# Block 0's first ff product as 26 products, its weight sums on GpSimd, and a new order of the side work of five stages

## The chip, the cores and the metric

The kernel runs on one core of a Trainium2 chip. Its time is device microseconds of one execution. All data are fp32. TensorE multiplies; VectorE, ScalarE and GpSimd do the rest; the DMA queues named here are issued from SyncE (SP) and ScalarE.

## The reference

A conditioned transformer block without attention, on x of shape (2, 2048, 512), with D = 512 and H = 1024 (`t` is the conditioning vector of a sequence):

```python
emb = jnp.dot(jax.nn.silu(t), ada_w) + ada_b
shift_msa, scale_msa, gate_msa, shift_mlp, scale_mlp, gate_mlp = jnp.split(emb, 6, axis=-1)
norm = _ln(x) * (1.0 + scale_msa[:, None]) + shift_msa[:, None]
h = jax.nn.gelu(jnp.dot(norm, ssm_w1) + ssm_b1, approximate=False)
ssm_out = jnp.dot(h, ssm_w2) + ssm_b2
x = x + gate_msa[:, None] * ssm_out
norm2 = _ln(x) * (1.0 + scale_mlp[:, None]) + shift_mlp[:, None]
hf = jax.nn.gelu(jnp.dot(norm2, ff_w1) + ff_b1, approximate=True)
ff_out = jnp.dot(hf, ff_w2) + ff_b2
x = x + gate_mlp[:, None] * ff_out
```

`_ln` is a layer norm without weights (eps 1e-6). ssm_w1 and ssm_w2 are 512x512, ff_w1 is 512x1024, ff_w2 1024x512.

## The kernel before

The 4096 rows are eight blocks of 512 tokens. Each block goes through four stages of TensorE, called here hA (norm times ssm_w1), oA (times ssm_w2, and the first residual), hC (second norm times ff_w1) and oC (times ff_w2, and the second residual), with the block's number behind them. The order of the stages is written out by hand: hA_0, oA_0, hA_1, oA_1, hC_0, hA_2, oC_0, hC_1 and so on, so that the side work of one block lies beside the products of another.

**Products.** A matrix product is done with fewer multiplications than the plain one, from sums and differences of quarters of its operands. `group` (L550, matmuls L565) does it with seven products, P1 to P7, in the order P1 P2 P6 P5 P7 P3 P4 (`ORDER`) or P1 P2 P5 P6 P7 P3 P4 (`FIRST`). A product of 512 x 512 quarters is four matmuls of the program, eight in the trace, and writes one of the PSUM banks y, x, v. `Second.products` (L1253, matmuls L1283) does the whole first ff product of a block in 26 products of half that size. Its operands are called registers: 28 of weights (16 pieces of ff_w1 and 12 of the room `fw1_s`, each 128x256) and some 24 of tokens. Two lists of sums over registers prepare them, `HK_A` (37 sums, weights, once) and `HK_B` (20 sums, tokens, per block), made by `sums_of_registers` (L1195). `HK_P` lists the products: bank, whether the bank starts afresh, the two registers, and which of the eight pieces of the result take the bank in, with signs. ScalarE reads a bank for the first time of a piece (L1297), VectorE adds to it later (L1300), and the gelu follows when a piece is complete (L1278). A bank must have been read before a product that starts it afresh or adds to it can run. Before, block 0 used `group` twice for hC_0 (14 products), and blocks 1 to 7 used `products`; the 37 weight sums were made on VectorE in hC_0, hA_2 and oC_0, after block 0 had used the plain ff_w1, and a quarter of ff_w1 that had been overwritten was loaded again (`fw1_quarter`).

**Side work.** A stage takes a table `hooks`, from the name of a product to the operations that are issued after it. What is issued goes to the queue of its engine and is done in that order. The side work is:

- `Norm`: the statistics of a block's rows, on VectorE (`stats`, L602, L603) or on ScalarE (`sums_on_act` L619, `squares_on_act` L631), then the root on GpSimd as a power (`root`, L649 to L656) with refinement steps (`rest`, L658 and L696 to L704 on VectorE, L671 on GpSimd), the normal form (`normal`, L719, ScalarE), turning by VectorE within 32x32 blocks (`turn`, L730) and a move of 16 DMA pieces of 64 KB (`move`, L739), the scale and shift of the conditioning (`modulate`, L767 on ScalarE, L769 on VectorE), and the sums of its quarters (`summed`, L386).
- The sums of the rows of a stage's result for the next one (`First.summed`, `Second.summed`; they use `cut_sum`, L386).
- The rows of emb: TensorE makes them (L287), VectorE shapes them (L329, L333), and the gates go to DRAM and come back (`store_gates` L364, `load_gate` and `take_gate` L374). The gate is multiplied into the rows of the second weight (`weight_of_second`, folds L434) and into its bias (`gb5_0` L1501), and seeds put the bias into PSUM (L529).

What sets the order near the change is this hand-written list, for the first stages, of what hangs on which product (L1443 to L1640).

Of the kernel before, what the change touches and what calls it, by code (L numbers as in the profile page):

```python
# [45 lines left out]
    (1, '-', 1, 0),  # L46
    (3, '+', 3, 1),
    (11, 'n', 10, 11),
    (27, '+', 11, 1),
    (26, '-', 27, 8),  # L50
    (25, '+', 13, 15),
    (25, '-', 25, 12),
    (24, '-', 27, 2),
    (23, '-', 3, 24),
    (8, '+', 8, 23),
    (8, '+', 0, 8),
    (22, '-', 12, 26),
# [51 lines left out]
    (5, True, 26, 20, ((5, -1), (7, 1))),  # L109
# [3 lines left out]
    (5, False, 8, 21, ((1, 1),)),  # L113
# [22 lines left out]

HK_BANK = {5: "y", 2: "x", 4: "v", 0: "x", 1: "y", 3: "v"}
# [3 lines left out]
def kernel(  # L141
# [447 lines left out]
    class Norm:  # L589
# [17 lines left out]
        def mixed_stats(self):  # L607

            sums, var = self.sums_on_act(), self.squares_on_act(D**-0.5)
            return sums[:3] + var[:4], self.stats(self.mv)[3:]  # L610

        def sums_on_act(self):
# [3 lines left out]
            self.unread = work.tile([P, C, D], F32, tag="blocks", name=f"unread{n}")  # L616
# [109 lines left out]
        def turn(self, c):  # L726
# [6 lines left out]
            )  # L733

# [460 lines left out]
    def sums_of_registers(program, reg, engs, copied=None, beside=()):  # L1195


        def op(n, d, f, a, b):
# [4 lines left out]
            elif f == "n":  # L1203
                nc.vector.scalar_tensor_tensor(reg[d], reg[a], -1.0, reg[b], ALU.mult, ALU.subtract)
            else:
                eng.tensor_tensor(reg[d], reg[a], reg[b], ALU.add if f == "+" else ALU.subtract)  # L1206
# [36 lines left out]
    class Second:  # L1243
# [9 lines left out]
        def products(self, fa, fb, hooks, act_first=False):  # L1253


            ends = {b: n for n, (b, *_) in enumerate(HK_P)}
            starts = [(n, b) for n, (b, fresh, *_) in enumerate(HK_P) if fresh]
            stops = set(ends.values())
            for n, b in starts:
                stops |= {max([m for m in range(n) if HK_P[m][0] == b], default=ends[b])}  # L1260
# [4 lines left out]
            left = [sum(d == r for (*_, rs) in HK_P for r, _ in rs) for d in range(8)]  # L1265
# [15 lines left out]
            for n, (b, fresh, ra, rb, reads) in enumerate(HK_P):  # L1281
# [171 lines left out]
    def gb2_0():  # L1453
        nc.vector.tensor_tensor(b2_bc, gate[2, 0], b2_bc, ALU.mult)

    def fold2(lo, hi):
        return [lambda k=k: found["w2"][1][k]() for k in range(lo, hi)]

    hooks = {}
    hook(hooks, ("P1",), n1_sums[2:3])  # L1460
    on_act, on_dve = n1[1].mixed_stats()
    hook(hooks, ("P1",), on_act)
    hook(hooks, ("P6",), on_dve + [n1[1].root, lambda: gate_rows_of(2)] + n1_sums[3:])
    hook(hooks, ("P6",), [n1[1].rest] + [lambda c=c: n1[1].normal(c) for c in range(2)])
    hook(hooks, ("P7",), [ssm_gate, gb2_0, lambda: seed("oA_0", b2_bc, 0), lambda: apart_row(b2_bc, nc.gpsimd)] + fold2(0, 1))
    hook(hooks, ("P3",), fold2(1, 2) + [lambda: n1[1].turn(0)] + fold2(2, 4))
    hook(hooks, ("P3",), fold2(4, 7) + [lambda: seed("oA_0", b2_bc, 1)])

    def later_loads():
        load_ada(5)  # L1470
        load_gate_b(5)
        load_w("fw2", fw2, fw2_sb)

    hA[0] = First(0, n1[0].ops, hooks, FIRST, hA_0)
    w2_ops = found["w2"][0]

    hA_sums = hA[0].summed(nc.vector, nc.gpsimd)
    n1[1].normal(2)
    n1[1].normal(3)
    run([hA_sums[0], lambda: n1[1].turn(1), hA_sums[1]])  # L1480
    hooks = {}
    hook(hooks, ("P1",), [lambda: n1[1].turn(2), lambda: n1[1].turn(3), lambda: n1[1].move((nc.sync, nc.scalar)), later_loads])
    hook(hooks, ("P1",), fold2(7, 8) + hA_sums[2:])
    hook(hooks, ("P1",), [lambda: found.update(pada=rows_of(3))])
    hook(hooks, ("P2",), [lambda: modulation(3, 0, found["pada"])])
    hook(hooks, ("P6",), [lambda: found.update(pada=rows_of(4))])
    hook(hooks, ("P4",), [lambda: modulation(3, 1, found["pada"])])
    hook(hooks, ("P7",), n1[1].moved((None, nc.vector)))
    n2 = {0: Norm(0, 2)}
    fw1_ops, fw1_sums, fw1_s = weight_of_first("fw1", fw1_sb)  # L1490
    hook(hooks, ("P2",), fw1_sums[:1])
    def ff_gate():
        take_gate(5, 0)
        gb[5] = load_row(work.tile([P, D], F32, tag="gb5", name="gb5_0", bufs=1), fb2)
        found["fw2"] = weight_of_second(fw2_sb, fw2_s, gate[5, 0], (nc.vector,), 4)

    def fold5(lo, hi):
        return [lambda k=k: found["fw2"][1][k]() for k in range(lo, hi)]

    def gb5_0():  # L1500
        nc.vector.tensor_tensor(gb[5], gate[5, 0], gb[5], ALU.mult)  # L1501
        apart_row(gb[5], nc.gpsimd)

# [4 lines left out]
    residual("oA_0", 0, hA[0], w2_ops, KD // 2, hooks, order=FIRST)
    run(st[2:])
    hooks = {}  # L1510
    hook(hooks, ("P1",), n1_sums[2:3])
    hook(hooks, ("P2",), n1_sums[3:] + on_dve + [n2[0].root])
    hook(hooks, ("P6",), [n2[0].rest] + [lambda c=c: n2[0].normal(c) for c in range(C)])
    hook(hooks, ("P5", "P7"), [lambda p=p: seed("oA_1", gb[2], p) for p in range(2)])
    hook(hooks, ("P5", "P7"), fw1_sums[1:3])
    hook(hooks, ("P6",), [lambda: gate_rows_of(5)])
    hook(hooks, ("P6", "P7", "P7", "P7"), [lambda c=c: n2[0].turn(c) for c in range(C)])
    hook(hooks, ("P7",), [lambda: n2[0].move((nc.sync,), (0, 1)), lambda: store_gates(5), lambda: load_gate(5, 0), lambda: store_gates(2)])
    load_x(2)
    hA[1] = First(1, n1[1].ops, hooks, FIRST)  # L1520

    n2[0].move((nc.scalar,), (2, 3))
    hA_sums = hA[1].summed(nc.vector)
    run(hA_sums[:2])
    n1[2] = Norm(2, 1)
    st = n1[2].stats()
    hooks = {}
    hook(hooks, ("P1",), hA_sums[2:3])  # L1530
    hook(hooks, ("P2",), hA_sums[3:] + fw1_sums[3:])
    hook(hooks, ("P2", "P6", "P6", "P5"), st)
    hook(hooks, ("P6",), n2[0].moved() + [ff_gate])
    n2_sums = n2[0].summed(nc.gpsimd)
    hook(hooks, ("P5",), n2_sums[:1] + [n1[2].scales])
    hook(hooks, ("P7",), n2_sums[1:] + [lambda c=c: n1[2].normal(c) for c in range(C)])
    hook(hooks, ("P7", "P3"), fold5(0, 2))
    turns = [lambda c=c: n1[2].turn(c) for c in range(C)]
    residual("oA_1", 1, hA[1], w2_ops, KD // 2, hooks)


# [392 lines left out]
```

## Time and profile before

| | us |
|---|---|
| median of 3 runs | 577.80 (577.78 to 578.07) |
| profiled execution | 577.74 |
| its span | 575.9 |
| hC_0, block 0's first ff product | 24.35 (68.19 to 92.54) |
| hC_1, block 1's, by 26 products | 22.45 (128.80 to 151.25) |

The page gives the busy time of each engine as a share of the span, the chain of work that ended last, and groups of instructions by line and tile. In a row of the timeline the first number is the start, the second the busy time of the row, both in us, then engine, line, operation, output from input, shapes and count; in brackets stands the idle time before it and what ended it. A row of the chain has start and length. A program matmul has two instructions in the trace, so x8 is a product of 512-size quarters.

### The profile page before, as it was taken

Reading aid. Unit: us, or ns where it says so; the run is one execution under the profiler, and the core shown is the slowest. Engines: PE = TensorE matmul, PEld = TensorE weight load, DVE = VectorE, ACT = ScalarE, POOL = GpSimd, SP = SyncE. Lnnn points to the kernel's source line nnn. Section 1 sums busy time; section 2 is a strip of 40 time slices with the busy share of each in tenths; the row PEclk is TensorE's granted clock in tenths of the full one; section 3 lists DMA queues with packets and bytes.
Section 4 is the critical chain, followed back from the end, with each engine's and each line's share of the span. In section 5 each row is a group of like instructions: output and inputs, shape, how many; then the busy total and the mean of one; then the engine's idle time right before and its main releaser. Section 6 shows DMA issues by size and latency. Waiting matters only on the chain.

```text
span 575.9 us, 10119 instructions
## 1 busy us (share of the span) xinstructions
PE 570.8 (99%) x3443; PEld 514.1 (89%) x3443; DVE 453.6 (79%) x963; ACT 292.7 (51%) x574; POOL 436.7 (76%) x460
## 2 busy tenths in 40 slices
PE   8999999999999999999999999999999999999997
PEld 4888888888899889998899988998889999899897
DVE  4968898996878586987869877996768598897676
ACT  3727457705652875448734588326655431742430
POOL 1665449999949869889898999998994885379361
PEclk9999999999999999999999999999999999999999
DMA  8977333303205223283032930243240240031002
GB/s 329 390 232 249 100 71 92 96 38 146 58 18 162 106 100 69 97 260 126 1 93 50 330 115 21 54 109 122 101 109 2 110 126 23 1 73 74 2 1 73
DMA packets 26863, 62.30 MB, mean 108 GB/s; under 512 B 5136, under 2 KB 6204, under 8 KB 25148
## 3 DMA queue, kind: packets, MB, share of 16 engines
q1 hardware_dynamic: 22784, 55.87, 29.9%
q10 hardware_dynamic: 4028, 5.79, 3.9%
q8 instruction: 27, 0.44, 0.4%
q14 instruction: 24, 0.20, 0.1%
HBM read 35.94 MB, written 9.97 MB: 80 GB/s over the span
## 4 chain that ended last, share of the span: by engine, by line
PE 97%; DMA 2%; SPq 0%; DVE 0%; issue 0%; DVEq 0%
PE px_hC L1283 11%; PE py_hA L565 10%; PE py_hC L1283 8%; PE pv_hC L1283 8%; PE pl_oC_P_y L1038 5%; PE py_oC L990 5%; PE pv_hA L565 5%; PE py_oA L925 5%; PE pl_oC_A_y L1133 4%; PE py_oA L565 4%; PE pl_oC_P_v L1038 3%; PE pl_oC_B_y L1133 3%; PE py_hC L565 2%; PE px_hA L565 2%; PE py_oC L565 2%; PE pl_oA_y L940 2%
## 5 line engine op out<-in xcount | busy, mean ns | idle before, releaser
L656 POOL TENSOR_TENSOR r<-ve,minus_half 128x4 f32<-128x4 f32 x16 | 16.6, 1037 | 57.7 <-DVE ve L655 50.7
L767 ACT ACTIVATE nT<-nT,mod,mod 128x512 f32<-128x512 f32 x32 | 23.4, 803 | 46.2 <-DMA nT<-blocks 16.3
L1206 POOL TENSOR_TENSOR forms<-forms 128x256 f32<-128x256 f32 x56 | 42.5, 759 | 3.8 <-DVE forms L1202 0.4
L1283 PE MATMUL py_hC<-forms,fw 128*128 128x256 f32 x168 | 40.9, 379 | 0.0
L1300 DVE TENSOR_TENSOR hClo<-hClo,py_hC 128x512 f32<-128x512 f32 x42 | 28.5, 683 | 11.6 <-ACT hClo L1297 8.2
L719 ACT ACTIVATE nT<-x,nmr,rstd 128x512 f32<-128x512 f32 x36 | 26.8, 803 | 19.4 <-DVE nmr L704 16.8
L1283 PEld LDWEIGHTS py_hC<-forms,fw 128*128 128x128 f32 x168 | 31.7, 190 | 4.6 <-DVE hClo L1300 0.2
L386 POOL TENSOR_TENSOR hSC<-hClo,hChi 128x512 f32<-128x512 f32 (+1 forms) x16 | 19.2, 1205 | 18.7 <-ACT hChi L1278 17.9
L602 DVE BATCH_NORM_STATS2 st<-x 128x6 f32<-128x512 f32 x42 | 28.4, 675 | 4.9 <-DMA x<-in_x_dram 4.9
L1300 DVE TENSOR_TENSOR hChi<-hChi,pv_hC 128x512 f32<-128x512 f32 x35 | 23.2, 678 | 9.2 <-PE pv_hC L1283 5.0
L1278 ACT ACTIVATE hClo<-hClo,colsT 128x256 f32<-128x256 f32 x56 | 25.3, 498 | 5.0 <-DVE hClo L1300 4.8
L1283 PE MATMUL px_hC<-forms,fw 128*128 128x256 f32 x112 | 27.6, 379 | 0.0
L767 ACT ACTIVATE x<-x,mod 128x512 f32<-128x512 f32 x24 | 17.5, 801 | 18.8 <-DMA x<-blocks 18.8
L386 POOL TENSOR_TENSOR hClo<-hClo 128x512 f32<-128x512 f32 (+1 forms) x23 | 26.5, 1154 | 0.0
L1278 ACT ACTIVATE hChi<-hChi,colsT 128x256 f32<-128x256 f32 x56 | 25.1, 496 | 1.9 <-DVE hChi L1300 1.9
L730 DVE STREAM_TRANSPOSE blocks<-nT 128x512 f32<-128x512 f32 x36 | 24.2, 695 | 1.7 <-ACT nT L719 1.7
L1297 ACT ACTIVATE hChi<-py_hC 128x512 f32<-128x512 f32 x14 | 7.6, 594 | 34.0 <-PE py_hC L1283 14.8
L1297 ACT ACTIVATE hClo<-px_hC 128x512 f32<-128x512 f32 x21 | 12.5, 596 | 22.5 <-PE px_hC L1283 18.9
L1283 PEld LDWEIGHTS px_hC<-forms,fw 128*128 128x128 f32 x112 | 21.3, 190 | 2.9
L565 PE MATMUL py_hA<-x,w 128*128 128x256 f32 x96 | 22.7, 379 | 0.0
L1300 DVE TENSOR_TENSOR hChi<-hChi,px_hC 128x512 f32<-128x512 f32 x28 | 19.1, 682 | 4.3 <-ACT hClo L1297 2.1
L1283 PE MATMUL px_hC<-forms,fw_s 128*128 128x256 f32 x84 | 20.5, 380 | 0.0
(537 smaller groups left out, 1921.9 us busy)
## 6 DMA issues: line engine op xcount, KB each, us to landing
x<-in_x_dram SPq DMA_DIRECT2D x13, 1024.0 KB
out_dram<-x SPq DMA_DIRECT2D x14, 512.0 KB
x<-blocks SPq DMA_DIRECT2D x96, 64.0 KB
nT<-blocks SPq DMA_DIRECT2D x88, 64.0 KB
ada<-in_L_cond_ada_w_dram SPq DMA_DIRECT2D x5, 1024.0 KB
fw<-in_L_cond_ff_w_dram SPq DMA_DIRECT2D x2, 2048.0 KB
nT<-blocks ACTq DMA_DIRECT2D x56, 64.0 KB
w<-in_L_cond_ssm_w_dram SPq DMA_DIRECT2D x2, 1024.0 KB
```

Of the source, the lines that this page charges most:

```text
L386: eng.tensor_tensor(out[:, r], a[:, r], b[:, r], f)
L565: nc.tensor.matmul(ps[b][j * apart][:, j, :], lhs(p, j, k), rhs(p, j, k), start=(fresh and j * (not apart) == 0 and k == 0), stop=(p in (" ...
L602: nc.vector.bn_stats(st, xs[self.i][:, c, :])
L767: nc.scalar.activation(dst, src, AF.Identity, bias=shift, scale=scale)
L925: nc.tensor.matmul(ps[BANK[p]][:, j, :], hops(p, j, k), wops[p][:, k, :], start=False, stop=(k == KD // 2 - 1), skip_group_check=True,)
L990: yield lambda j=j, k=k: nc.tensor.matmul(ps[BANK[p]][:, j, :], hops(p, j, k), wops[p][:, k, :], start=False, stop=(k == kdim - 1), skip_g ...
L1038: nc.tensor.matmul(t[:, n, :], hops.leaves[p][f][:, k, :], leaf_wops[p][f][:, k, :], start=room not in started, stop=(f in ("P2", "P3", "P ...
L1133: nc.tensor.matmul(rooms[g, b][:, at[p], :], hops.leaves[p][f][:, k, :], leaf_wops[p][f][:, k, :], start=(g, b) not in started, stop=(f in ...
L1206: eng.tensor_tensor(reg[d], reg[a], reg[b], ALU.add if f == "+" else ALU.subtract)
L1278: nc.scalar.activation(h, h, AF.Gelu_apprx_tanh, bias=fb1T[:, m : m + 1])
L1283: nc.tensor.matmul(ps[b][:, j, :], fa[ra][:, j * P : (j + 1) * P], fb[rb].rearrange("p a (c q) -> p c a q", q=Q), start=(fresh and j == 0) ...
L1300: nc.vector.tensor_tensor(dest(d), dest(d), ps[b], op)
```

## The change

Block 0's ff product is done with `products` too. The signs in `HK_A`, `HK_B` and `HK_P` are changed so that no sum is of the form -a-b (which VectorE alone could do, L1204), so that any engine can make any sum. `HK_P0` is `HK_P` in another order, for block 0. The 37 weight sums move ahead of hC_0, to oA_0, hA_1, oA_1 and hC_0: five on VectorE (the first four and the last), 32 on GpSimd. The token sums of block 0 are made in oA_1 and hC_0, four on VectorE and 16 on GpSimd. The reload of ff_w1's quarter and the four Strassen sums of ff_w1 go.

The hooks of six stages are no longer written as calls but as a table `PLAN`, stage to product to names of operations, and a table `BY`, name to engines, a letter for each operation (V, A, G for VectorE, ScalarE, GpSimd). Moves are split at the pieces `ON_SCALAR` between SP and ScalarE's queue. The statistics of block 0's second norm are cut into parts (`split_stats`). The last steps for block 2's first norm move from GpSimd to VectorE (`root`), its sums stay on GpSimd, and one of its four statistics goes to ScalarE. Gate 5's rows are taken into use in hC_0, at product 15, and its folds are in hC_0 and hA_2; the sums of ff_w2 and of the hidden rows of block 0 are in hA_2. The second norm of block 1 is modulated, and its token sums begin, in oC_0.

```diff
 HK_A = [
-    (1, '-', 1, 0),
-    (3, '+', 3, 1),
-    (11, 'n', 10, 11),
+    (1, '-', 0, 1),
+    (3, '-', 1, 3),
+    (11, '+', 10, 11),
...
+HK_P0 = [HK_P[n] for n in (1, 0, 2, 6, 9, 4, 5, 3, 8, 11, 7, 12, 13, 14, 15, 10, 16, 19, 18, 17, 20, 22, 21, 23, 25, 24)]
+PLAN = {
+    "hA_0": {
+        "start": "n1_0.sum.0 n1_0.sum.1",
+        "P1": "n1_1.stats.0 n1_1.stats.1 n1_1.stats.2 n1_1.stats.3 n1_0.sum.2 n1_1.stats.6",
+        "P2": "n1_1.stats.4 n1_1.stats.5",
+        "P6": "n1_1.stats.7 n1_1.root.0 gate_2.0 n1_0.sum.3 n1_1.rest.0 n1_1.normal.0",
...
+        "P3": "w2.1 w2.2 n1_1.turn.0 w2.3 w2.4 w2.6 w2.5",
+        "P4": "n1_1.normal.1 n1_1.normal.3 n1_1.normal.2 seed_0.1",
+    },
+    "oA_0": {
+        "start": "hA_0.sum.0 rows.0 n1_1.turn.1 hA_0.sum.1",
...
+        "P5": "a.0",
+        "P6": (
+            "rows.1 a.1 a.2 a.3 a.4 a.5 a.6 a.7"
+            " a.8 a.9 a.11 a.12 mods.0"
+        ),
+        "P7": "n1_1.modulated.0 n1_1.modulated.1 mods.1 n1_1.modulated.3 n1_1.modulated.2",
...
+    "hA_1": {
+        "start": "a.14 n2_0.stats.4 n2_0.stats.3 n2_0.stats.6 n2_0.stats.7",
+        "P1": "a.13 a.15 seed_1.1 seed_1.0 n2_0.stats.8 n2_0.root.0",
+        "P2": "n1_1.sum.2 a.16 a.17 a.18 a.19 a.21 a.22 a.23",
+        "P6": (
+            "a.20 n2_0.rest.0 n2_0.normal.0 n2_0.normal.1 n2_0.normal.2 gates.0 rows.2 n2_0.normal.3"
+            " n1_1.sum.3"
+        ),
+        "P7": "a.24 n2_0.turn.0 n2_0.turn.1",
+        "P3": "n2_0.turn.2 n2_0.turn.3 gates.1 n2_0.move.0",
+        "P4": "a.26 n1_2.stats.0",
+    },
+    "oA_1": {
+        "start": "hA_1.sum.0 a.29 hA_1.sum.2 n1_2.stats.1 n2_0.move.1",
+        "P1": "hA_1.sum.1 n1_2.stats.2 gates.2 a.28 n1_2.stats.4 n1_2.stats.3 hA_1.sum.3",
+        "P6": "n1_2.stats.5 n1_2.root.0",
+        "P5": "a.25 n2_0.modulated.0",
+        "P7": (
+            "n2_0.modulated.1 n2_0.modulated.2 n2_0.modulated.3 copies.0 b.0 b.2 b.1 b.3"
+            " b.4 b.6 b.5 b.7"
+        ),
+        "P3": (
+            "b.8 b.9 b.10 b.11 b.13 n1_2.rest.0 b.15 b.12"
+            " a.27 a.31 b.16 b.17 a.30 a.32"
+        ),
+        "P4": "table.0",
+    },
+    "hC_0": {
+        0: "n1_2.normal.0 a.33 b.14",
+        1: "n1_2.turn.0 n1_2.normal.1",
+        2: "b.19 n1_2.normal.3",
+        3: "b.18 n1_2.normal.2 n1_2.turn.1",
+        4: "a.34",
+        5: "n1_2.turn.2",
+        6: "n1_2.turn.3",
+        7: "a.35",
+        8: "n1_2.move.1 n2_1.stats.0 n1_2.move.0",
+        9: "a.36",
...
+        15: "ff_gate.0",
...
+        19: "fw2.0 n1_2.modulated.2 n1_2.modulated.1 n1_2.sum.0 n1_2.sum.2 n1_2.sum.1",
+        20: "n1_2.sum.3 fw2.4",
+        22: "n2_1.normal.0 n2_1.normal.1",
+        23: "gb_5.0 gb_5.1 fw2.1",
+        25: "n2_1.turn.0",
+    },
+    "hA_2": {
+        "start": "n2_1.normal.3",
...
+        "P6": "fw2.2 fw2.6 hC.sum.0 hC.sum.4 n2_1.turn.1 fw2.8",
+        "P5": "hC.sum.1 hC.sum.2 seed_2.1 fw2.9 hC.sum.5",
...
+BY = {
...
+    "n1_2.sum": "GGGG",
+    "hA_0.sum": "VVGG",
+    "hA_1.sum": "VVGG",
...
+    "n1_1.modulated": "AAVV",
+    "n2_0.modulated": "VAAV",
...
+    "a": "VVVVGGGGGGGGGGGGGGGGGGGGGGGGGGGGGGGGV",
+    "b": "VVVGGGVGGGGGGGGGGGGG",
+}
+BESIDE, COPIED, ON_SCALAR, ON_ACT = (17,), (1,), (8, 7, 2), ((), ('P5',))
...
-            self.early = (self.i, self.which) in ((2, 1), (1, 2))
+            self.early = (self.i, self.which) == (1, 2)
...
+        def move_some(self, eng, pieces):
+            for a, m in pieces:
+                eng.dma_start(
+                    out=self.nT[m * Q : (m + 1) * Q, a, :],
+                    in_=self.bl[a * Q : (a + 1) * Q, m].rearrange("p k c q -> p (k c q)"),
+                )
...
+    residual("oA_0", 0, hA[0], w2_ops, KD // 2, begin("oA_0"), order=FIRST)
+    hooks = begin("hA_1")
+    hA[1] = First(1, n1[1].ops, hooks, FIRST, on_act=ON_ACT[0])
+    residual("oA_1", 1, hA[1], w2_ops, KD // 2, begin("oA_1"))
+    hooks = begin("hC_0")
+    hC.products(fa, fb[0], hooks, True, HK_P0)
```

In the table, `a` are the weight sums in the order of `HK_A`, `b` the token sums in that of `HK_B`, `n1_1` is block 1's first norm, `n2_0` block 0's second, `w2` and `fw2` the folds and sums of the second weights, `loads` and `gates` DMAs.

More of the change, by code (lines that the diff above doesn't have):

```diff
@@ L1264, in products @@
             }
-            left = [sum(d == r for (*_, rs) in HK_P for r, _ in rs) for d in range(8)]
+            left = [sum(d == r for (*_, rs) in products for r, _ in rs) for d in range(8)]
             fresh_dest, done = set(range(8)), []
@@ L1451, in ssm_gate, with rows_for @@
         found["w2"] = weight_of_second(w2_sb, w2_s, gate[2, 0], (nc.vector,))
[L1453 to L1491, printed above, removed]
+    def rows_for(g):
+        found[g] = rows_of(g)
     def ff_gate():
@@ L1508 @@
[L1508 to L1517, printed above, removed]
@@ L1533 @@
[L1533 to L1539, printed above, removed]
-    hC = Second(0)
-    n2[1] = Norm(1, 2)
-    hooks = {}
-    hook(hooks, ("P1", "P1", "P2"), turns)
@@ new lines @@
+    at("seed_0", lambda: seed("oA_0", b2_bc, 0), lambda: seed("oA_0", b2_bc, 1))
+    at("seed_1", lambda: seed("oA_1", b2_bc, 0), lambda: seed("oA_1", b2_bc, 1))
+    at("w2", *[lambda n=n: found["w2"][1][n]() for n in range(8)])
+    at("loads", lambda: load_ada(5), lambda: load_gate_b(5), lambda: load_w("fw2", fw2, fw2_sb), lambda: load_x(2))
+    later("hA_0.sum", 4, lambda: hA[0].summed(ENGS["hA_0.sum"]))
+    later("hA_1.sum", 4, lambda: hA[1].summed(ENGS["hA_1.sum"]))
+    at("rows", lambda: rows_for(3), lambda: rows_for(4), lambda: gate_rows_of(5))
@@ new lines @@
+    at("b", *[lambda n=n: form_0(n) for n in range(len(HK_B))])
+    at("table", lambda: nc.scalar.activation(unread, minus_half, AF.Gelu_apprx_tanh))
+    room = forms[:, 8:].rearrange("p (c n) a r -> p c (n a r)", c=C)
+    later("n1_2.stats", 6, lambda: sum(n1[2].mixed_stats(1, room), []))
+    at("n1_2.root", n1[2].root)
+    at("n1_2.rest", n1[2].rest)
+    turned("n1_2", n1[2], ON_SCALAR[2], ENGS["n1_2.normal"])
+    at("n1_2.modulated", *n1[2].moved(ENGS["n1_2.modulated"]))
+    later("n1_2.sum", 4, lambda: n1[2].summed(ENGS["n1_2.sum"]))
@@ new lines @@
+    later("n2_1.stats", 4, n2[1].stats)
+    at("n2_1.scales", n2[1].scales)
+    turned("n2_1", n2[1], 0, ENGS["n2_1.normal"])
+    at("ff_gate", ff_gate)
+    at(
+        "gb_5",
+        lambda: nc.vector.tensor_tensor(gb[5], gate[5, 0], gb[5], ALU.mult),
+        lambda: apart_row(gb[5], nc.gpsimd),
+    )
+    at("fw2", *[lambda n=n: found["fw2"][1][n]() for n in range(12)])
+    at("seed_2", lambda: seed("oC_0", gb[5], 0), lambda: seed("oC_0", gb[5], 1))
+    later("hC.sum", 8, lambda: hC.summed(0, nc.gpsimd) + hC.summed(1, nc.gpsimd))
@@ L1623 @@
         hooks = {}
-        if i == 1:
-            assert not fa_sums
         if i == 1:
```

276 lines of the change are left out of this document (158 added, 118 removed).

## The prediction

> **What bounds the kernel now.** I read the page first, then the idle time of TensorE, then the chain of waits in order of time, and after that the timeline of each other engine between 20 and 95 us.
>
> ```profile
> span 575.9 us, 10119 instructions
> PE 570.8 (99%) x3443; PEld 514.1 (89%) x3443; DVE 453.6 (79%) x963; ACT 292.7 (51%) x574; POOL 436.7 (76%) x460
> PE 97%; DMA 2%; SPq 0%; DVE 0%; issue 0%; DVEq 0%
> ```
>
> ```profile
> PE idle L1392 <- POOL w_t masks.py:199: 1.3, 1, 1.3
> PE pada L304 <- DMA ada<-in_L_cond_ada_w_dram: 0.3, 1, 0.3
> ```
>
> TensorE is 97% of the chain, and its two waits lie at the start. Every matmul less is a gain of its whole length, and every wait that the new order makes for TensorE is a loss of its whole length. Of the chain these rows matter (start, length, what):
>
> ```profile
> 42.76 1.73 PE py_hA L565 x8
> ...
> 50.68 1.92 PE py_hA L565 x8
> ...
> 59.51 1.73 PE py_oA L565 x8
> ...
> 62.96 1.73 PE py_oA L565 x8
> ...
> 68.19 1.73 PE py_hC L565 x8
> ...
> 75.10 1.90 PE py_hC L565 x8
> ...
> 92.54 1.73 PE py_hA L565 x8
> ...
> 125.35 3.45 PE py_oC L565 x16
> ...
> 151.25 1.73 PE py_oA L565 x8
> ```
>
> Block 0's first ff product runs from 68.19 to 92.54, 24.35 us in 14 products. Block 1's, already in 26 half-size products, runs from 125.35 + 3.45 = 128.80 to 151.25, 22.45 us. The sum is made against the profiled execution, 577.74 us (1.84 outside its span, taken as unchanged); the median of the runs is 577.80, 0.06 above.
>
> **1. The products.** 14 x 4 = 56 program matmuls become 26 x 2 = 52: 22.45 for 24.35, **-1.90**. Of this, 1.73 is four matmuls (one row of eight instructions) and 0.17 the long product at 75.10. It needs every sum and every bank in time; the rest of the sum goes through these.
>
> **2. Weight sums on GpSimd.** Four sums of 128x1024 go, and 37 sums of 128x256, which VectorE made between 84 and 128 us, come 50 us earlier: five on VectorE (four early, the last in the ff stage), 32 on GpSimd.
>
> ```profile
> 35.49 1.27 POOL L386 TENSOR_TENSOR hSA<-forms,hSA 128x512 f32<-128x512 f32 x1
> 36.72 2.35 POOL L386 TENSOR_TENSOR fw_s<-fw 128x1024 f32<-128x1024 f32 x1
> 48.72 1.02 POOL L656 TENSOR_TENSOR r<-ve,minus_half 128x4 f32<-128x4 f32 x1 [9.64 <-DVE ve L655]
> ```
>
> ```profile
> L1206 POOL TENSOR_TENSOR forms<-forms x56: 722/729/1195, 118.5 to 531.8; 128x256 f32<-128x256 f32 x56
> L1206 DVE TENSOR_TENSOR fw_s<-fw x4: 683/901/1377, 93.3 to 120.4; 128x256 f32<-128x256 f32 x4
> L1206 DVE TENSOR_TENSOR fw_s<-fw,fw_s x5: 833/843/950, 99.4 to 113.7; 128x256 f32<-128x256 f32 x5
> L1206 DVE TENSOR_TENSOR fw<-fw_s,fw x2: 407/428/448, 115.6 to 122.7; 128x256 f32<-128x256 f32 x2
> ```
>
> The columns are least, median and greatest ns. GpSimd's first 12 must wait for VectorE's fourth, which I place at 38.2. At 0.73 each, plus about 0.7 for VectorE's sums beside them, they end at 47.6. Behind them in GpSimd's queue stands the power for block 0's second norm (r of the row at 48.72), which then ends at 49.45, not 49.74: still no loss. Eleven more follow, and the two sums of block 1's hidden rows on GpSimd end at 59.5 and 61.5, needed at 62.96 and a product later. The last weight sum ends at about 84.4, its product is due at about 88. Cost **0** as long as a sum takes 0.73; rival C is what happens otherwise.
>
> That VectorE and GpSimd hold each other up is in these rows: 0.43 us on VectorE alone, 0.84 to 1.38 beside GpSimd. The Trainium skill, SBUF — State Buffer, section "SBUF: two separate sides", calls the port pair of the two an exclusive lock: a VectorE instruction with two SBUF inputs against a GpSimd instruction that reads SBUF, and the later one waits out the whole of the other. The trace agrees: 1.38 is 0.43 and a wait of 0.95, most of the 1.27 us of a GpSimd 128x512 sum. By that rule every such sum of VectorE may wait one GpSimd sum; rival D is that case, priced from the rows.
>
> **3. Block 1's first norm (hA_0).** ScalarE now loads its gelu table and does one gelu ahead of two squares of the statistics.
>
> ```profile
> 21.43 1.28 ACT L842 ACT_TABLE_LOAD   x1
> ...
> 41.00 1.52 ACT L767 ACTIVATE nT<-nT,mod 128x512 f32<-128x512 f32 x2 [10.42 <-DMA fw_t<-in_L_cond_ada_b_dram]
> ```
>
> ```profile
> 22.63 0.17 DVE L655 TENSOR_SCALAR ve<-mv 128x4 f32<-128x4 f32 x1
> ...
> 30.79 1.15 DVE L386 TENSOR_TENSOR hSA<-hSA,forms 128x512 f32<-128x512 f32 x1
> ...
> 32.46 1.29 DVE L730 STREAM_TRANSPOSE blocks<-nT 128x512 f32<-128x512 f32 x2
> ...
> 48.47 0.17 DVE L655 TENSOR_SCALAR ve<-mv 128x4 f32<-128x4 f32 x1
> ...
> 53.50 1.88 DVE L730 STREAM_TRANSPOSE blocks<-nT 128x512 f32<-128x512 f32 x3
> ...
> 57.38 0.69 DVE L386 TENSOR_TENSOR hSA<-hSA,hA 128x512 f32<-128x512 f32 x1
> ```
>
> ve moves from 22.63 to 23.4, the last turn ends at 34.45 instead of 33.75, the 16 pieces land 0.65 later than the 41.00 at which both engines begin to modulate. The second chunk is ready at 43.2; hA_1's first product (42.76) reaches it 0.43 in, at 43.19. **+0.1** (0 to 0.3).
>
> **4. hA_1.** ve of block 0's second norm still waits for ScalarE's last square (48.2 against 48.47 for ve before). What is new is behind it on VectorE's queue: two reads of finished products and a sum of 128x512 that the product at 50.68 needs. These end at about 50.8: **+0.15**. If the sum takes 1.15 as at 30.79 instead of 0.69, 0.65; if ScalarE is earlier, 0.
>
> **5. oA_1.** The four turns now end at 56.85 (55.38 before: 53.50 + 1.88), because VectorE's sums come before them. Behind them are two sums of the hidden rows. Before, GpSimd was idle there and the second took 0.69; now it is busy, so I take 1.15 for each: ready at 59.95, due at 59.51 plus the 0.25 lost so far. **+0.2** (0 if at 0.69; 0.9 if each waits a further 0.35).
>
> **6. The move of block 0's second norm.** It is split nine pieces on SP and seven on ScalarE's queue; gate 5's four stores now stand ahead of it on SP.
>
> ```profile
> 55.44 4.95 SPq L739 DMA_DIRECT2D nT<-blocks  x8
> 60.44 2.72 SPq L364 DMA_DIRECT2D gates<-w_t  x4
> ```
>
> ```profile
> 57.60 4.14 ACTq L739 DMA_DIRECT2D nT<-blocks  x6
> 63.29 2.93 ACT L767 ACTIVATE nT<-nT,mod,mod 128x512 f32<-128x512 f32 x4 [5.94 <-DMA gates<-w_t]
> ...
> 69.29 2.93 ACT L719 ACTIVATE x<-x,nmr,rstd 128x512 f32<-128x512 f32 x4 [1.38 <-POOL nmr L671]
> ...
> 129.76 1.09 ACT L1297 ACTIVATE hChi<-py_hC 128x512 f32<-128x512 f32 x2 [14.81 <-PE py_hC L1283]
> ```
>
> The stores take 2.72 but are issued from 52.3, while VectorE still turns: hidden. The pieces go out from 57.0 to 63.0 (0.62 each on SP, 0.69 on ScalarE's queue) and land 1.55 after the last issue, as before (57.60 + 4.14 to 63.29): 64.55 against 63.29. Two engines modulate until 66.35, four instead of 2.93 us of one. The 20 token sums, 16 of them on GpSimd with two weight sums between, follow from 66.35: with 0.73 a sum the ones due for products 6, 9 and 12 of the new order (counted from 0, the stage starting at 68.6) are ready 0.1, 0.5 and 0.7 early. **0** (0 to 0.5: at 0.84, the median row beside the other engine, the first is 0.5 late).
>
> **7. hC_0 itself.** In its first 6 us ScalarE makes two reads, the four normals of block 2's norm and two more reads: at 0.55 and 0.73 each they end 5.8 us in. VectorE's third turn waits for the last normal, and in its queue the read of product 6, whose bank product 8 overwrites, stands behind it.
>
> ```profile
> 72.74 1.28 DVE L730 STREAM_TRANSPOSE blocks<-x 128x512 f32<-128x512 f32 x2
> ...
> 130.63 1.29 DVE L1300 TENSOR_TENSOR hChi<-hChi,pv_hC 128x512 f32<-128x512 f32 x2 [0.97 <-PE pv_hC L1283]
> ```
>
> A turn and a read are 0.64 each: the read ends 7.2 to 7.3 us in, product 8 is due at 8 x 22.45 / 26 = 6.91. **+0.4** (0 if ScalarE's reads come earlier; 1.0 if another read gets between). Later banks come free in time by the same count. Gate 5's rows, its eight folds and the four fw2 sums with the eight hidden sums on GpSimd (4 x 2.35 + 8 x 1.27) now reach into hA_2 and oC_0; the first product that needs them is due 3 us after they are ready. The 512 KB reload of weights on ScalarE's queue goes, which nothing waited for. The move of block 2 has 14 of 16 pieces on SP and lands near 88, 0.4 ahead of the sum that needs it. **0** (0 to 0.6).
>
> **Sum:** 577.74 - 1.90 + 0.10 + 0.15 + 0.20 + 0.40 = 576.69, **576.7 us**. With all stalls at their low ends 575.84; with all at their high ends (0.3, 0.65, 0.9, 0.5, 1.0, 0.6) 579.8.
>
> **The rivals.**
> A is the sum above.
> B: all of it is hidden. The stalls that I foresee are each under half a microsecond and rest on hand-counted queues; an operation 0.2 us earlier removes two of them. 577.74 - 1.90 = 575.84. Against it: four places would all have to be kind.
> C, the slower side: the power for block 0's second norm falls behind the twelve weight sums. From 38.2 to the 48.45 at which it is to start is 10.25 us, 0.85 per sum. GpSimd's greatest row is 1195 ns; at 1.07, between that and the 0.95 that VectorE's sums reach, the power starts at 51.0, 2.6 late, and so do the turns, the sums of item 5, and with them oA_1: 576.7 + 2.6 = 579.3. It decides (579.3 is past +0.2%) from 2.2 us on, 1.04 per sum. For it: GpSimd has no gap there any more, where it waited 9.64 before. Against it: the median is 0.729, and VectorE has only two sums of two SBUF inputs in that time.
> D: the port waits of item 2 come in full. VectorE's sum in hA_1 waits one GpSimd sum (0.15 + 0.73), both of item 5 0.73 instead of 0.46 (0.2 + 0.54), items 3 and 7 stay (0.5): 2.12, 577.74 - 1.90 + 2.12 = 578.0.
>
> **How the numbers follow.** 0.2% is 1.16 us, about what a measurement of this kernel tells from no change: faster is below 576.6, slower above 578.9. A 0.42 (its own range 576.2 to 577.2, so half of it counts as faster), B 0.23, D 0.18, C 0.17. Faster 0.23 + 0.20 = 0.43, same 0.22 + 0.18 = 0.40, slower 0.17. The range leaves out C and ends between D and C: 575.8 to 578.7.
>
> **What would show it.** In the changed profile: 26 products of 0.86 in hC_0, 22.45 us and what stalls add; the power for block 0's second norm starting at 48.5 (C: 50.6 or later); VectorE's sums of item 5 at 1.15 (B: 0.69, D: 1.4); the modulation at 64.5; idle TensorE of 0.1 to 0.4 us at hA_1's start and its fifth product, oA_1's third, and product 8 of hC_0. The prediction is wrong if TensorE waits somewhere else, above all for token sums after 74 us, or in hA_2 and oC_0, where I count nothing.

## The result and the profile after

The changed kernel takes 579.44 us (median of 11 runs, 579.28 to 580.41), the kernel before 577.80 (11 runs): a ratio of 1.0028, 95% interval 1.0019 to 1.0037. It is 0.28% slower; the interval excludes no change, and its lower end lies just under the 0.2% that the prediction took as the limit of a measurement. The forecast was 576.7 with a range to 578.7.

The profiled execution after takes 579.28 us, 1.54 more than the one before; its page begins:

```profile
span 577.5 us, 10112 instructions
PE 569.3 (99%) x3435; PEld 512.0 (89%) x3435; DVE 439.6 (76%) x954; ACT 295.8 (51%) x585; POOL 451.0 (78%) x475
```

TensorE is busy for 1.5 us less, and yet the span is 1.6 us longer. TensorE's waits (line, what it waited for, us in total, times, longest) tell why:

```profile
PE idle L1512 <- POOL w_t masks.py:199: 1.3, 1, 1.3
PE py_hA L672 <- DVE hA L957: 1.3, 2, 1.0
PE pada L409 <- DMA ada<-in_L_cond_ada_w_dram: 0.9, 1, 0.9
PE py_oA L672 <- DVE hSA L491: 0.6, 1, 0.6
```

The first and third lie at the start, where hA_0 begins at the same time as before. The second and fourth are new. A table by stage (length, PE busy, PEld, DVE, ACT, POOL, granted clock, DMA share, GB/s) puts them in place. The stages are hA_1, oA_1, hC_0 and hA_2; first the kernel before:

```profile
42.60:55.89 13.29, 13.29 (x89) 11.37 (x88) 11.72 (x28) 9.42 (x21) 7.17 (x4) 1.00 0.78 277
55.89:68.03 12.14, 12.14 (x58) 10.56 (x56) 8.85 (x19) 4.88 (x8) 3.66 (x6) 1.00 0.45 109
68.03:92.38 24.35, 24.35 (x114) 21.20 (x112) 21.99 (x39) 15.81 (x25) 15.58 (x27) 1.00 0.27 69
92.38:104.47 12.09, 12.09 (x58) 10.64 (x57) 11.61 (x15) 7.19 (x14) 12.09 (x14) 1.00 0.41 100
```

and the same four of the kernel after:

```profile
42.88:56.54 13.66, 13.37 (x90) 11.37 (x88) 12.03 (x27) 10.38 (x24) 13.08 (x17) 1.00 0.76 276
56.54:69.48 12.94, 12.35 (x57) 10.56 (x56) 11.22 (x23) 5.96 (x12) 8.51 (x10) 1.00 0.41 103
69.48:92.58 23.10, 22.96 (x106) 19.51 (x104) 21.90 (x45) 13.51 (x25) 18.16 (x31) 1.00 0.25 57
92.58:105.91 13.33, 12.32 (x57) 10.56 (x56) 10.85 (x17) 10.75 (x21) 13.17 (x11) 1.00 0.01 1
```

hA_1 starts 0.28 later; then hA_1 +0.37, oA_1 +0.80, hC_0 -1.25, hA_2 +1.24: oC_0 starts 1.44 later, and everything behind it keeps that distance. hC_0 did win its 1.9 (22.45 and 0.65 of waits). The five stages around it (0.28 of it in hA_0 and oA_0) lost 2.69, and hC_0 itself 0.65.

The rows of VectorE after, at the places where TensorE waits:

```profile
23.31 0.17 DVE L773 TENSOR_SCALAR ve<-mv 128x4 f32<-128x4 f32 x1 [0.83 <-ACT unread L749]
23.52 0.29 DVE L446 TENSOR_TENSOR w_t<-pada,fw_t 128x128 f32<-128x128 f32 x1
...
48.23 0.57 DVE L773 TENSOR_SCALAR ve<-mv 128x4 f32<-128x4 f32 x1 [1.39 <-ACT unread L749]
...
58.47 0.69 DVE L1012 TENSOR_TENSOR x<-py_oA,x 128x512 f32<-128x512 f32 x1 [0.82 <-PE py_oA L672]
59.08 1.62 DVE L491 TENSOR_TENSOR hSA<-hSA,hA 128x512 f32<-128x512 f32 x1
...
75.54 0.70 DVE L848 STREAM_TRANSPOSE blocks<-x 128x512 f32<-128x512 f32 x1
76.17 0.65 DVE L1420 TENSOR_TENSOR hChi<-hChi,px_hC 128x512 f32<-128x512 f32 x1
```

The gate's rows (w_t) stand behind ve, which waits for ScalarE: 23.52 for 22.86. In hA_1 ve waits 1.39 for ScalarE with four steps behind it that the fifth product needs. In oA_1 the second hidden sum starts behind the read of P1 and takes 1.62. In hC_0 the read of product 6 ends at 76.8 and product 8 starts at 76.87. And the chain of waits through the start of hA_2, in order of time:

```profile
88.51 1.52 ACT x L893 x2
90.03 0.80 ACT hChi L1398 x2
90.83 1.41 ACT x L893 x2
92.24 0.80 ACT hClo L1398 x2
93.04 0.80 ACT hChi L1398 x2
93.84 0.71 ACT nT L837
...
94.58 0.71 DVE blocks L848
95.29 1.17 DVE nT L841
96.46 0.61 DVE hA L957
...
97.20 1.97 PE py_hA L672 x8
```

The read of P1 (L957) was free to start at about 94.4, when P1 was done. It stands behind a turn (L848), which waits for ScalarE's normal form, and behind a normal form on VectorE (L841).

### The profile page after: what moved, and what is told of

Read it like the earlier page. It is cut to its first block, busy times and chain, and to the rows that moved or that the text cites. A ratio compares the mean times of both kernels' runs of the same rounds, so it can differ in the third digit from the quotient of the medians.

```text
span 577.5 us, 10112 instructions
## 1 busy us (share of the span) xinstructions
PE 569.3 (99%) x3435; PEld 512.0 (89%) x3435; DVE 439.6 (76%) x954; ACT 295.8 (51%) x585; POOL 451.0 (78%) x475
## 4 chain that ended last, share of the span: by engine, by line
PE 90%; DMA 2%; SPq 2%; DVE 2%; ACT 2%; issue 0%; DVEq 0%; ACTq 0%
PE px_hC L1403 11%; PE py_hA L672 9%; PE py_hC L1403 9%; PE pv_hC L1403 9%; PE pl_oC_P_y L1164 5%; PE py_oC L1116 5%; PE py_oA L1051 4%; PE pv_hA L672 4%; PE pl_oC_A_y L1259 4%; PE pl_oC_P_v L1164 3%; PE pl_oC_B_y L1259 3%; PE py_oA L672 3%; PE py_oC L672 2%; PE pl_oA_y L1066 2%; SPq L856 2%; PE pl_oC_A_v L1259 2%
## 5 line engine op out<-in xcount | busy, mean ns | idle before, releaser
L1330 POOL TENSOR_TENSOR forms<-forms 128x256 f32<-128x256 f32 x64 | 47.9, 749 | 6.5 <-DVE forms L1330 2.3
L1403 PE MATMUL py_hC<-forms,fw 128*128 128x256 f32 x192 | 46.7, 379 | 0.0
L1403 PEld LDWEIGHTS py_hC<-forms,fw 128*128 128x128 f32 x192 | 36.3, 190 | 5.2 <-DVE hClo L1420 0.2
L491 POOL TENSOR_TENSOR hSC<-hClo,hChi 128x512 f32<-128x512 f32 x14 | 18.2, 1302 | 18.6 <-ACT hChi L1398 17.8
L1403 PE MATMUL px_hC<-forms,fw 128*128 128x256 f32 x128 | 31.5, 379 | 0.0
L1398 ACT ACTIVATE hClo<-hClo,colsT 128x256 f32<-128x256 f32 x64 | 28.8, 498 | 5.0 <-DVE hClo L1420 4.8
L1398 ACT ACTIVATE hChi<-hChi,colsT 128x256 f32<-128x256 f32 x64 | 28.7, 496 | 3.8 <-DVE hChi L1420 3.8
L848 DVE STREAM_TRANSPOSE blocks<-nT 128x512 f32<-128x512 f32 x36 | 24.2, 694 | 1.9 <-ACT nT L837 1.9
L1403 PE MATMUL px_hC<-forms,fw_s 128*128 128x256 f32 x96 | 23.6, 382 | 0.1
L1403 PE MATMUL pv_hC<-nT,fw 128*128 128x256 f32 x96 | 23.3, 379 | 0.0
L1420 DVE TENSOR_TENSOR hClo<-hClo,px_hC 128x512 f32<-128x512 f32 x26 | 17.6, 677 | 7.0 <-PE px_hC L1403 6.6
```

The source lines that it names most:

```text
L491: eng.tensor_tensor(out[:, r], a[:, r], b[:, r], f)
L1398: nc.scalar.activation(h, h, AF.Gelu_apprx_tanh, bias=fb1T[:, m : m + 1])
L1403: nc.tensor.matmul(ps[b][:, j, :], fa[ra][:, j * P : (j + 1) * P], fb[rb].rearrange("p a (c q) -> p c a q", q=Q), start=(fresh and j == 0) ...
L1420: nc.vector.tensor_tensor(dest(d), dest(d), ps[b], op)
```

## The experiments

Each stands against the kernel after (579.44) and shares its runs of the kernel before (577.78 to 577.80) with those measured beside it. Ratios are to the kernel before.

**turn_later.**

```diff
-        25: "n2_1.turn.0",
+        25: "",
...
-        "P1": "seed_2.0 fw2.3",
+        "P1": "n2_1.turn.0 seed_2.0 fw2.3",
```

> The first turn of block 1's second norm goes from product 25 of hC_0 to behind the read of P1 in hA_2; nothing else changes. Theory 1 (VectorE's queue: the read of P1, which the third product of hA_2 needs, stands behind a turn that waits for ScalarE): the read ends before 95.8 us, TensorE's wait of 1.0 at hA_2's third product goes, oC_0 starts 1.0 to 1.25 earlier, 579.4 becomes 578.2. Theory 2 (ScalarE is late and sets hA_2 anyway: its normals come behind a move that lands at 88 and behind gelus): the wait comes back at the read of P1, behind the normal form on VectorE, or at the move of block 1's second norm, and the time stays within 0.3 of 579.4.

578.73 us, 1.0018 (1.0009 to 1.0027). hA_2 takes 12.54 instead of 13.33. The queue was the cause of 0.79. Of the 0.45 that are left, TensorE waits 0.2 for GpSimd's second sum of block 2's quarters, and VectorE's normal form still stands ahead of the read. Theory 1, with a smaller gain than it gave.

**s1_first.**

```diff
-        "start": "hA_1.sum.0 a.29 hA_1.sum.2 n1_2.stats.1 n2_0.move.1",
-        "P1": "hA_1.sum.1 n1_2.stats.2 gates.2
+        "start": "hA_1.sum.0 hA_1.sum.1 a.29 hA_1.sum.2 n1_2.stats.1 n2_0.move.1",
+        "P1": "n1_2.stats.2 gates.2
```

> The second sum of block 1's hidden rows (oA_1) is issued ahead of the read of P1 on VectorE instead of behind it. Theory 1 (order: behind the read it could not begin before 59.08): it ends by 59.3, TensorE's wait of 0.6 at oA_1's third product goes, hC_0 starts 0.75 earlier, 578.7. Theory 2 (port: beside GpSimd's sums it takes 1.6 us wherever it stands): it ends at 59.5 or later and a wait of at least 0.2 stays. Theory 3 (the token sums of hC_0, which start from the landing of block 0's second norm, set the end): oA_1 is 0.75 shorter and hC_0 as much longer, the time stays within 0.2 of 579.4.

578.60 us, 1.0014 (1.0005 to 1.0023). The sum runs from 57.70 to 58.81, the wait is gone, hC_0 starts 0.83 earlier. Of that hC_0 gives 0.25 back: it takes 23.35, since product 6 comes earlier than its token sum on GpSimd (a wait of 0.4). Theory 1, with a part of theory 3.

**gate_first.**

```diff
-"n1_1.stats.7 n1_1.root.0 gate_2.0 n1_0.sum.3
+"n1_1.stats.7 gate_2.0 n1_1.root.0 n1_0.sum.3
```

> The rows of gate 2 are issued ahead of the root of block 1's first norm in hA_0, so that VectorE's work on them does not stand behind a step that waits for ScalarE's last square. Theory 1 (that queue set TensorE's wait ahead of the gate's rows): the rows start at 23.75 instead of 23.96, hA_1 starts 0.25 to 0.3 earlier, 579.15. Theory 2 (the move of block 1's first norm, landing at 41.5, sets hA_1's start): the 0.3 comes back as a wait at hA_1's first product, time unchanged.

579.71 us, 1.0035 (1.0022 to 1.0048), 0.27 above the kernel after. Rows of TensorE in it:

```profile
22.73 1.99 PE L672 MATMUL py_hA<-nT,w 128*128 128x256 f32 x8
24.56 1.05 PE L453 MATMUL pgate<-w_t,fw_t 128*128 128x128 f32 x8
...
43.73 2.18 PE L672 MATMUL py_hA<-nT,w 128*128 128x256 f32 x8
45.76 1.89 PE L672 MATMUL px_hA<-nT,w 128*128 128x256 f32 x8
```

and of the three other engines:

```profile
24.24 0.69 DVE L491 TENSOR_TENSOR nS<-nT,nS 128x512 f32<-128x512 f32 x1
...
26.59 0.68 DVE L974 TENSOR_TENSOR forms<-py_hA,forms 128x512 f32<-128x512 f32 x1
...
24.41 1.39 POOL L774 TENSOR_TENSOR r<-ve,minus_half 128x4 f32<-128x4 f32 x1 [2.31 <-DVE ve L773]
...
42.78 1.52 ACT L893 ACTIVATE nT<-nT,mod 128x512 f32<-128x512 f32 x2 [9.73 <-DMA fw_t<-in_L_cond_ada_b_dram]
```

In the kernel after, the power on GpSimd was this row:

```profile
23.57 1.02 POOL L774 TENSOR_TENSOR r<-ve,minus_half 128x4 f32<-128x4 f32 x1 [2.25 <-DVE ve L773]
```

This execution was 0.84 late already when hA_0 began (14.61 for 13.77), so only distances count. The gate's rows no longer wait (24.56 is 1.83 behind the product before them, 2.08 after), but hA_0 and oA_0 together still take 29.12. VectorE now issues the sum nS right behind ve, ahead of the power, and the power takes 1.39 instead of 1.02. The read behind it (L974), counted from the start of hA_0, comes 0.37 later, and TensorE loses 0.16 at the last product of hA_0 (27.33), 0.10 at the rows of emb behind it and 0.10 in oA_0 (38.48). The turns and the move are later by as much, and hA_1's second product comes 2.03 behind the first, not 1.73: the modulation of its rows still goes on until 44.3, 0.57 into the first. So theory 1 is refuted, and the move can hold up hA_1 as theory 2 says. But the edit itself made that path longer, so this run does not show how long it was in the kernel after. An estimate: of an overlap of 0.57 here 0.30 were lost, of 0.65 in no_weight_sums 0.37, so all beyond 0.28 is lost. Without the gate's wait hA_1 would begin at about 42.57 in the kernel after, where the modulation ends at 43.08, 0.51 later: about 0.23 of the 0.3 would have been lost there anyway.

**ve_later.**

```diff
-        "P1": "a.13 a.15 seed_1.1 seed_1.0 n2_0.stats.8 n2_0.root.0",
-        "P2": "n1_1.sum.2 a.16
+        "P1": "a.13 a.15 seed_1.1 seed_1.0 n2_0.stats.8",
+        "P2": "n2_0.root.0 n1_1.sum.2 a.16
```

> In hA_1 the step of block 0's second norm that waits for ScalarE's last square (ve) stands behind the read of P2 on VectorE instead of ahead of it. Theory 1 (order): the reads of P5 and P6 end 0.55 earlier, at 50.55, TensorE's wait of 0.3 at hA_1's fifth product goes, oA_1 starts 0.35 earlier, and the power on GpSimd starts at most 0.2 later; 579.1. Theory 2 (GpSimd's sums beside it hold up VectorE's sum of the same row, the place of ve does not matter): the wait stays above 0.2, time unchanged.

578.50 us, 1.0014 (1.0005 to 1.0023). The fifth product of hA_1 is on time, as theory 1 says, and oA_1's wait went with it, which neither theory gave: GpSimd's sums now fall otherwise, and the second hidden sum takes 0.68 from 58.73, issued 0.03 ahead of a GpSimd sum of 128x256 that takes 1.23 instead of 0.73. hC_0 starts 1.20 earlier.

**no_weight_sums.**

```diff
-    at("a", *sums_of_registers(HK_A, fa, ENGS["a"]))
+    at("a", *sums_of_registers(HK_A, fa, ENGS["a"])[:4], *[lambda: None] * 33)
+    fa[16:] = fa[:11] + fa[:1]
```

> The 32 weight sums on GpSimd and the last one on VectorE are left out (the products take other weights in their place, so the ff products are not the right ones; their number, shapes and order are the same). It takes away whatever those sums do to VectorE's sums and to GpSimd's own queue. Theory 1 (order of VectorE's queue): the wait at hA_1's fifth product stays at 0.25 to 0.3, because ve waits for ScalarE either way; oA_1's third product waits at most 0.1, because the second hidden sum then takes 0.7 instead of 1.6 but still starts behind the read of P1; hA_2's 1.0 stays: 578.5 to 578.7. Theory 2 (port and GpSimd's queue make the waits of hA_1, oA_1 and hC_0): all four waits ahead of hA_2 go, 577.5 or less.

578.12 us, 1.0010 (1.0001 to 1.0019). The two rows of VectorE that answer to 48.23 and 59.08 above:

```profile
48.34 0.17 DVE L773 TENSOR_SCALAR ve<-mv 128x4 f32<-128x4 f32 x1 [1.38 <-ACT unread L749]
...
59.15 0.68 DVE L491 TENSOR_TENSOR hSA<-hSA,hA 128x512 f32<-128x512 f32 x1
```

ve still waits 1.38 for ScalarE, but takes 0.17 instead of 0.57, and the hidden sum starts at the same time and takes 0.68 instead of 1.62. oA_1 does not wait any more, hC_0 starts 0.78 earlier, hA_2 keeps its 1.0. hA_1's fifth product does not wait either: what follows ve starts 0.30 earlier (48.42 for 48.72), and the product itself is due 0.36 later, since 0.37 were lost at the second. Which of the two it needed is not separated. So oA_1's wait needed both: the place behind the read (s1_first) and GpSimd's sum beside it. Neither theory alone.

**short_sum_beside.**

```diff
-        "start": "hA_1.sum.0 a.29 hA_1.sum.2 n1_2.stats.1 n2_0.move.1",
+        "start": "hA_1.sum.0 a.29 n1_2.stats.1 n2_0.move.1",
...
-gates.2 a.28 n1_2.stats.4
+gates.2 a.28 hA_1.sum.2 n1_2.stats.4
```

> On GpSimd alone, the hidden sum of 128x512 that ran from 58.88 to 60.15, beside VectorE's second hidden sum (59.08, 1.62 long), changes places with the weight sum of 128x256 behind it. VectorE's order is untouched. Theory 1 (VectorE's sum waits out the whole GpSimd instruction that began before it): beside a 0.73 sum it waits to about 59.6 and ends at 60.2 to 60.3, TensorE's wait at oA_1's third product falls from 0.59 to about 0.15, hC_0 starts 0.45 earlier, 579.0. Theory 2 (the two share the port by halves, or the sum is long for another reason): it still takes 1.4 or more, the wait stays above 0.35, time unchanged.

578.82 us, 1.0018 (1.0009 to 1.0027). oA_1 takes 12.39 instead of 12.94. hC_0 starts only 0.22 earlier, since hA_1's fifth product waits 0.53 in this execution, 0.29 after. VectorE's sum, and GpSimd's rows beside it:

```profile
59.41 1.06 DVE L491 TENSOR_TENSOR hSA<-hSA,hA 128x512 f32<-128x512 f32 x1
```

```profile
59.20 0.73 POOL L1330 TENSOR_TENSOR fw_s<-fw 128x256 f32<-128x256 f32 x1
59.88 1.72 POOL L491 TENSOR_TENSOR hA<-hA 128x512 f32<-128x512 f32 x1
```

In the kernel after, GpSimd's rows there were these:

```profile
58.88 1.27 POOL L491 TENSOR_TENSOR hA<-hA 128x512 f32<-128x512 f32 x1
60.10 1.18 POOL L1330 TENSOR_TENSOR fw_s<-fw 128x256 f32<-128x256 f32 x1
```

After, VectorE's sum was issued 0.20 into a GpSimd sum of 1.27 and ended 0.55 behind its end (60.70). Here it was issued 0.21 into one of 0.73 and ended 0.54 behind its end (60.47); the next GpSimd sum, issued at 59.88, took 1.72 instead of 1.27. The one issued later waits out the rest of the other's instruction, so what VectorE pays depends on the length of the GpSimd sum that it meets. Theory 1. The Trainium skill, SBUF — State Buffer, section "SBUF: two separate sides", says that the one that starts first holds the ports shared by the two for its whole instruction, and the other blocks. The trace agrees: in both runs VectorE's sum ends the same 0.54 to 0.55 behind GpSimd's.

**three_moves** puts ve_later, s1_first and turn_later together.

> Three edits together: ve behind the read of P2 in hA_1, the second hidden sum at the start of oA_1, the first turn of block 1's second norm behind the read of P1 in hA_2. If the gains lie at different waits of TensorE: hC_0 starts at 68.3 (one gain of 1.2, the first two meet there), hA_2 takes 12.5, oC_0 starts at 104.0 to 104.1, 577.7 to 577.8, level with the kernel before. If the waits only move on: 578.4.

577.56 us, 0.9998 (0.9989 to 1.0007): level with the kernel before. hC_0 starts at 68.31, hA_2 takes 12.44, as expected; hC_0 takes 23.44, and its longest wait (0.5) is for product 6's token sum.

**five_moves** adds this to three_moves:

```diff
-        18: "n1_2.modulated.3",
-        19: "fw2.0 n1_2.modulated.2 n1_2.modulated.1 n1_2.sum.0 n1_2.sum.2 n1_2.sum.1",
+        18: "n1_2.modulated.3 n1_2.modulated.2 n1_2.modulated.1",
+        19: "fw2.0 n1_2.sum.0 n1_2.sum.1 n1_2.sum.2",
...
-        "start": "n2_1.normal.3",
-        "P1": "n2_1.turn.0 seed_2.0 fw2.3",
+        "start": "",
+        "P1": "n2_1.normal.3 n2_1.turn.0 seed_2.0 fw2.3",
```

> The three moves, and in addition for hA_2: the normal form of rows 3 on VectorE behind the read of P1, the second sum of block 2's quarters ahead of the third on GpSimd, and all four modulations of block 2 ahead of ScalarE's gelus. If hA_2's rest of 0.45 (its 12.5 against 12.09) is these two queues: hA_2 takes 12.1, 577.3. If not, hA_2 stays at 12.5, 577.7.

577.91 us, 1.0002 (0.9993 to 1.0011), a miss. hA_2's third product is on time, but its fifth now waits 0.8: the normal form and the turn stand ahead of the reads of P2 and P6 instead. hA_2 takes 13.15.

**seven_moves** adds to that `"b": "VVVVGGV..."` for `"VVVGGGV..."` and block 2's third turn from product 5 to product 6.

> The five moves, and in addition for hC_0: the fourth token sum on VectorE instead of GpSimd, and block 2's third turn behind the read of product 6 instead of ahead of it. If hC_0's 0.65 over 22.45 are the two waits I see in the trace (product 6 for a token sum, product 8 for the read of its bank): hC_0 takes 22.5 to 22.6, 576.7 to 576.8, the prediction's 576.7. If block 2's move, now 0.65 later, sets hA_2: hA_2 takes 12.7, 577.2.

578.61 us, 1.0016 (1.0007 to 1.0025), a miss. Products 6 and 8 are on time. Product 3 now waits for a read of block 1's rows behind the added sum (0.3), product 10 for the reads of product 7 behind two turns (0.4): hC_0 takes 23.79.

**best_a** is three_moves, the two edits of five_moves at products 18 and 19, and:

```diff
-            " b.4 b.6 b.5 b.7"
+            " b.4 b.6 b.5 b.7 b.11"
...
-            "b.8 b.9 b.10 b.11 b.13
+            "b.8 b.9 b.10 b.13
...
-        "start": "n2_1.normal.3",
+        "start": "",
...
-        "P5": "hC.sum.1 hC.sum.2 seed_2.1
+        "P5": "hC.sum.1 hC.sum.2 n2_1.normal.3 seed_2.1
```

> The three moves, and: the token sum of product 6 right behind the one that it reads (three places earlier on GpSimd), in hA_2 the normal form of rows 3 behind the read of P6, the second sum of block 2's quarters ahead of the third, and block 2's modulations ahead of ScalarE's gelus. If the 0.64 at hC_0's product 6 in three_moves is GpSimd's order alone, product 6 is on time; product 8 then waits for the read of product 6, which stands behind a turn until 75.05, by 0.4 to 0.5: hC_0 23.1 to 23.2 instead of 23.44, hA_2 12.1, 576.9. If a token sum further on becomes late (product 7 needs one that is now after it), hC_0 stays at 23.4 and the time at 577.2.

577.15 us, 0.9988 (0.9979 to 0.9997): 0.12% faster than the kernel before, which the interval just tells from no change. hC_0 takes 23.10: product 6 is on time, and product 8 waits 0.48 for the read behind the turn, as expected. hA_2 takes 12.44 and not 12.1, which is a miss: its sixth product waits 0.25.

**best_b** is best_a with block 2's third turn after product 7 and its fourth after product 8.

> As best_a, with block 2's third and fourth turns one after product 7 and one after product 8, behind the reads of products 6 and 7. If product 8's wait was the turn ahead of that read: hC_0 22.5 to 22.7; block 2's move starts 1.9 later and lands at 89, and what hA_2 loses by it tells whether the move has slack: none lost, 576.3; 1 us lost, 577.3.

579.15 us, 1.0026 (1.0016 to 1.0036), a miss. Product 8 is on time, but ScalarE's two DMA issues, ahead of its read of product 9, now wait for the later turn:

```profile
78.55 1.40 ACTq L856 DMA_DIRECT2D x<-blocks  x2
80.00 0.60 ACT L1417 ACTIVATE hClo<-py_hC 128x512 f32<-128x512 f32 x1 [5.81 <-DVE fw L1330]
```

The product that needs the bank waits 0.6. The modulations come later too, and in hA_2 TensorE waits 0.9 for ScalarE's read of P5. That is the price of a late move, which I had put on its landing.

**best_c** is best_a with `seed_2.0` moved from P1 to P5 of hA_2.

> As best_a, with the first seed of oC_0 on ScalarE behind the read of P5 in hA_2 instead of ahead of it. If the 0.25 that hA_2's sixth product still waits in best_a is ScalarE's read of P5 behind that seed (0.58): the read ends 0.58 earlier, hA_2 takes 12.1 instead of 12.44, 576.8. If VectorE's normal form and turns set the same product: 577.1.

577.00 us, 0.9988 (0.9979 to 0.9998). hA_2 takes 12.15, so ScalarE's queue was that wait. It gains 0.79 over the kernel before, where hC_0's 26 products alone would give 1.9; what is lost is the 0.65 in hC_0, of which 0.48 lie at product 8, about 0.3 ahead of hA_1, and smaller pieces.

## Why the prediction was wrong

The forecast was -1.05, the profiled executions differ by +1.54. The step that failed most is the 0 for the stages behind hC_0 in item 7: hA_2 lost 1.24, a place that the prediction itself had named as a sign of being wrong. Next come oA_1 (0.80 for 0.20), hC_0 (0.65 for 0.40), hA_1 (0.37 for 0.15) and hA_0 (0.31 for 0.10). By its own steps:

1. **Products, -1.90.** Right. hC_0 is 22.45 and its waits.
2. **Weight sums, 0.** Right for GpSimd's own queue, with less room than counted: the first twelve sums run from 38.82 to 48.78 (forecast 38.2 to 47.6), the power starts at 48.89, not 48.45, and the last weight sum ends at 85.5. That cost nothing, since VectorE takes up the power's result only at 51.38. The step failed in that it priced only GpSimd's lateness; what the sums do to VectorE was left to steps 4 and 5, at 0.46 a sum.
3. **hA_0, +0.10.** Measured 0.31 (29.11 for 28.80 from the start of hA_0 to that of hA_1). The cause, ScalarE's gelu ahead of the squares, was right. I followed it only through the move, whose modulation ended at 43.08 (43.2 forecast) and cost nothing by itself; the loss came at the gate's rows, which the same late ve held up. gate_first took that wait away and lost as much elsewhere in hA_0 and oA_0, and by the estimate there the move would have cost about 0.23 next.
4. **hA_1, +0.15.** Measured 0.37, same place, same cause: undersized by ve, 0.57 long beside GpSimd.
5. **oA_1, +0.20.** Measured 0.80. Right place, wrong reading of the queue. The item's own terms do not give its 59.95: two sums of 1.15 from 56.85 end at 59.15, and the 0.80 between is not named. The second sum stands behind the read of P1, which I left out, so it could not start before 59.08; and beside a sum of 128x512 it paid 0.94 over its 0.68, not 0.46, the value from a single row.
6. **Move and token sums, 0.** The modulation starts at 64.8 (64.55 forecast) and ends at 67.38 (66.35 forecast), and hC_0 gains a wait of only 0.1 at product 6. That is luck: hC_0 started at 69.48, where the item counted on 68.6. In s1_first and three_moves, where it starts at 68.65 and 68.31, product 6 waits 0.4 and 0.5 for its token sum, the high end of the range.
7. **hC_0, +0.40, and the stages behind it, 0.** hC_0's waits are 0.65, the largest, 0.30, at product 8 with the cause that I gave. hA_2, where I wrote 0 (0 to 0.6), costs 1.24, the largest loss. I asked whether block 2's moved rows come in time for its own sums, and did not walk VectorE's queue at the start of hA_2, where the read of P1 stands behind a turn and a normal form of another block.

Rival C gave 579.3, close to the time, but not by its mechanism: the power was 0.4 late and not 2.6, and nothing waited for it. Rival D named the port wait: it is real, in oA_1, larger for one sum than D's 0.73 and nearly absent at the others (the first hidden sum took 0.64). B is refuted. best_a and best_c, 0.12% faster, show that the change can pay a little; with the same products and sums, the order of the side work set the sign.

Not settled: why the load that rowsT waits for at the start came late in the profiled execution of gate_first (rowsT waits 0.92 for it and starts at 8.77, for 6.80 after), why the modulation in no_weight_sums starts at 42.08 for 41.56, and the 0.17 of hC_0's 0.65 in best_c that do not lie at product 8.

## What to carry to other kernels

Walk every in-order queue across every stage that a change reorders, not only the stage that gets shorter: each read of a finished product must stand ahead of whatever waits for another engine. Where several paths end close together, shortening one gives little, and a gain at one wait can move the next one up. Moving a step out of the way of one read puts it ahead of another: look at the next two reads on that queue, and at the DMA issues that wait for it.

## What the hardware showed that I had not expected

The price of a VectorE sum beside a GpSimd sum goes to the one issued later, and it is close to the rest of the other: for the same 128x512 sum, VectorE took 0.68 us alone, 1.62 with 1.07 of a GpSimd sum left, and 1.06 with 0.52 left. Issued 0.03 ahead in ve_later, VectorE took 0.68 and GpSimd paid. That holds for a step with a single tensor input too: ve, of 128x4, took 0.57 instead of 0.17 beside the weight sums, and the modulation of two chunks 1.42 (L895, at 41.62) instead of the 1.01 that it takes without them. The power on GpSimd paid too, 1.39 instead of 1.02, when VectorE's sum was issued ahead of it (gate_first).
